# Grouped-query stages: where a step's softmax factors are finished, and how its values are shared out over four slots

## The chip, the cores and the metric

The kernel runs on one core of a Trainium2 chip as one launch. The core has five engines that work on their own instruction streams and meet through semaphores: TensorE (matrix products; its weight loads are shown apart), VectorE, ScalarE, GpSimd and SyncE, which here issues most of the DMA transfers. The metric is the device time of one execution in microseconds; less is better.

## The reference, cut to what matters

Four layers, each an attention over a context of 1601 positions and then a feed-forward part, on x of 4 x 256 x 256 in float32. Layers 1 and 3 have grouped-query attention: 16 query heads of width 128 that share 4 key/value heads. Layer 1 also attends to its own 256 positions and rotates queries and keys by position; layer 3 attends to the context alone:

```python
q = rms_norm((h @ Wq).reshape(B, S, 16, 128), q_norm_w)
k = rms_norm((e @ Wk).reshape(B, S_enc, 4, 128), k_norm_w)
v = (e @ Wv).reshape(B, S_enc, 4, 128)
k, v = jnp.repeat(k, 4, axis=2), jnp.repeat(v, 4, axis=2)
scores = jnp.einsum('bqhd,bkhd->bhqk', q, k) * 128**-0.5
probs = jax.nn.softmax(scores, axis=-1)
out = jnp.einsum('bhqk,bkhd->bqhd', probs, v).reshape(B, S, 16 * 128) @ Wo
```

The other stages (an attention that keeps the best 54 keys, mixtures of experts, a linear layer, an attention over image and text keys) are not touched.

## The kernel before, in words

The stages run one after the other. `gqa` is called twice, for layer 1 with rotation tables (`"l1a"`) and for layer 3 without them (`"l3a"`). Keys run in chunks of 128: 15 of them in the first (1857 keys), 13 in the second (1601); the last has 65.

A stage has 16 units (4 batches x 4 key/value heads); a unit has four steps (two blocks of 128 query positions x two pairs of heads). A step takes its scores in four slots, two score tiles in each. The order of the work is written out by hand: TensorE, ScalarE, VectorE and GpSimd get their instructions exactly in the order in which Python issues them. A loop over slots t issues the slot's scores (L1242) and then, phase by phase, what was put on that slot's lists:

```python
for phase in ("first", "early", "mid", "late", "last", "values", "pe", "post"):
    if phase == "mid" and rest:
        rest()
    for f in todo.pop((t, phase), ()):
        f()
```

Within a list the order is that in which entries were put there. The production of keys and queries (`begin`) is entered before the loop; `combine(i)` and `values(i)` are entered when the loop reaches t = 4i.

What one step i does, with its slots:

- Scores, slots 4i-4 to 4i-1: four products for four groups of 32 keys go into one of three PSUM score tiles (L1242). `rest` takes the negative maximum on VectorE (L1250) and the exponential with its sum on ScalarE (L1251). Each partition has a quarter of the keys, so a row's four quarters have maxima and sums of their own.
- Slot 4i: `turn` (L1264, TensorE) brings maxima and sums of the quarters onto 8 partitions; `top` takes the common maximum and the exponential of the difference (L1269, L1271 on VectorE, L1272 on ScalarE).
- Slot 4i+1: `total`, four small VectorE operations (L1276 to L1279), makes factors out of these; `back` (L1283, TensorE) turns the factors back; at the slot's end VectorE copies them (L1288) and GpSimd multiplies the first half of the step's exponentials by them (L1291, `scale(0)`). The second half follows in slot 4i+2.
- Slots 4i+3 and 4i+4: two block transposes on VectorE (L1296, `blocks`), in phase "last", write PT.
- Slots 4i+6 to 4i+9: the product of values and PT (L1322), chunk by chunk, into the one accumulator bank; slot 4i+10 copies it out on ScalarE (L1329), and after every second step the output projection follows (L1335).

So several steps overlap: the slot 4i+1 that has step i's `back` has the last part of the values of step i-2.

Beside this, keys, values and queries of the next unit are produced in the slots: projections (L1111, L1185) in phase "pe"; in the next slot "early" sums of squares on ScalarE (L1119, L1192), on VectorE ssq (queries, L1194) and rsq_t (L121), then the power on GpSimd (L122), and copies of V; "late" the scaling (L1127, L1202, L1206), in the first layer a slot later the rotation on GpSimd and VectorE (L1158 to L1160), then the transposes (L1137, L1217), and in the following slot, "early", the copies of KT and QT (L96 on VectorE, L98 on ScalarE, by turns). In the second stage the keys and values of the first batch and most of the second are loaded, not produced, so its slots have less TensorE work there.

PSUM has eight banks in these stages: three for scores, four (`tr`) for projections and transposes in rotation, one accumulator (`acc`).

Of the kernel before, what the change touches and what calls it, by code (L numbers as in the profile page):

```python
# [52 lines left out]
def kernel(ctx: ExitStack, tc: tile.TileContext, A, out: bass.AP):  # L53
# [5 lines left out]
    def ps_tile(shape, tag):  # L59
        return pools["ps"].tile(shape, F32, tag=tag, name=tag, bufs=pools[tag])  # L60
# [4 lines left out]
    def ps_tr():  # L65
        return ps_tile([P, 512], "tr")

    def ps_acc():
        return ps_tile([P, 512], "acc")

    def small(shape, tag, bufs=4):
        return sm.tile(shape, F32, tag=tag, name=tag, bufs=bufs)
# [107 lines left out]
    def residual(j, ps):  # L180
        nc.vector.tensor_tensor(X[j], ps, X[j], ALU.add)
# [383 lines left out]
    def sort_constants(pool):  # L565
        def table(shape, pattern, base, tag):
            t = pool.tile(shape, F32, tag=tag, name=tag)
            nc.gpsimd.iota(t, pattern, base=base, channel_multiplier=0, allow_small_or_imprecise_dtypes=True)
            return t

        k = dict(
            before=table([P, E], [[ROOM, E]], -1, "k_before"),
            first=table([P, E], [[ROOM, E]], P, "k_first"),
            step=table([P, E - 1], [[P, E - 1]], P, "k_step"),
            expert=table([P, E], [[1, E]], 0, "k_expert"),
            more=table([P, MORE], [[1, MORE]], 0, "k_more"),
            tri8=table([P, E, E], [[1, E], [-1, E]], 0, "k_tri8"),
        )
        nc.vector.tensor_scalar(k["tri8"], k["tri8"], 0.0, 1.0, ALU.is_ge, ALU.mult)
        k["tri"] = pool.tile([P, P], F32, tag="k_tri", name="k_tri")  # L580
        make_upper_triangular(nc, k["tri"], val=1.0, diag=True)
        k["ones"] = pool.tile([P, P], F32, tag="k_ones", name="k_ones")
        nc.gpsimd.memset(k["ones"], 1.0)
        return k
# [423 lines left out]
    def gqa(xT, key, tabs=None, early=None, others=None):  # L1008
        rope = tabs is not None
        ch = chunks(NCTX + (S if rope else 0))  # L1010
        nch = len(ch)
# [3 lines left out]
        W = nch * 32  # L1015
        lens = [sum(max(0, min(32, n - 32 * r)) for _, n in ch) for r in range(4)]
        pairs = [ch[i : i + 2] for i in range(0, nch, 2)]
        units = B * KVH
        steps = [(u, tt, pr) for u in range(units) for tt in range(2) for pr in range(2)]
        ET = mybir.EngineType  # L1020
        with (
# [11 lines left out]
            for i in range(3):  # L1033
                t = ps_tile([P, 512], f"sc{i}")
# [11 lines left out]
            def at(slot, phase, *fs):  # L1046
                todo.setdefault((slot, phase), []).extend(fs)
# [207 lines left out]
            def combine(i):  # L1255

                pes, ms = state.pop(steps[i])
                v = {}
                t = 4 * i

                def turn():
                    tr = ps_tr()
                    for k in range(2):
                        nc.tensor.transpose(tr[0:8, k * P : (k + 1) * P], ms[:, k, :], ident)  # L1264
                    v["m"], v["s"] = (tr[0:8, k * P : (k + 1) * P].rearrange("p (r t) -> p r t", r=4) for k in range(2))

                def top():
                    v["top"] = small([P, 32], "top", 2)[0:8]
                    nc.vector.tensor_reduce(v["top"], v["m"].rearrange("p r t -> p t r"), AX.X, ALU.min)  # L1269
                    v["f"] = pool.tile([P, 4, 32], F32, tag="cf", name="cf")[0:8]  # L1270
                    nc.vector.tensor_tensor(v["f"], v["top"].unsqueeze(1).to_broadcast([8, 4, 32]), v["m"], ALU.subtract)  # L1271
                    nc.scalar.activation(v["f"], v["f"], AF.Exp)  # L1272

                def total():
                    fs = pool.tile([P, 4, 32], F32, tag="cfs", name="cfs")[0:8]
                    nc.vector.tensor_tensor(fs, v["f"], v["s"], ALU.mult)  # L1276
                    nc.vector.tensor_reduce(v["top"], fs.rearrange("p r t -> p t r"), AX.X, ALU.add)
                    nc.vector.reciprocal(v["top"], v["top"])
                    nc.vector.tensor_tensor(v["f"], v["f"], v["top"].unsqueeze(1).to_broadcast([8, 4, 32]), ALU.mult)  # L1279

                def back():
                    v["tr"] = ps_tr()
                    nc.tensor.transpose(v["tr"][:, 0:8], v["f"].rearrange("p r t -> p (r t)"), ident[0:8, 0:8])  # L1283

                def scale(g):
                    if g == 0:
                        v["fac"] = small([P, 8], "fac", 2)
                        nc.vector.tensor_copy(v["fac"], v["tr"][:, 0:8])  # L1288
                    for a in range(4):
                        w = pes[g][:, a, :]  # L1290
                        nc.gpsimd.tensor_scalar(w, w, v["fac"][:, g * 4 + a : g * 4 + a + 1], 1.0, ALU.mult, ALU.mult)  # L1291

                def blocks(g):
                    if g == 0:
                        state[steps[i]] = pool.tile([P, nch, 2 * P], F32, tag="PT", name="PT")
                    nc.vector.transpose(  # L1296
                        state[steps[i]][:, :, g * P : (g + 1) * P].rearrange("p k (a t) -> p a k t", a=4),
                        pes[g].rearrange("p a (k i) -> p a k i", k=nch),
                    )

                at(t, "early", turn)
                at(t, "late", top)
                at(t + 1, "early", total)
                at(t + 1, "pe", back)
                at(t + 1, "post", lambda: scale(0))
                at(t + 2, "late", lambda: scale(1))
                at(t + 3, "last", lambda: blocks(0))
                at(t + 4, "last", lambda: blocks(1))

            def values(i):  # L1310
                u, tt, pr = steps[i]
                j = u // KVH * 2 + tt
                t = 4 * i + 6
                v = {}

                def part(q):
                    if q == 0:
                        v["ps"] = ps_acc()
                    V, PT = state[u]["V"], state[steps[i]]
                    for k in range(q * 4, min(q * 4 + 4, nch)):  # L1320
                        n = ch[k][1]
                        nc.tensor.matmul(  # L1322
                            v["ps"][:, 0 : 2 * P], V[:n, k, :], PT[:n, k, :], start=(k == 0), stop=(k == nch - 1)
                        )

                def out():
                    if pr == 0:
                        state["OT"] = pool.tile([P, GRP * P], F32, tag="OT", name="OT")
                    nc.scalar.copy(state["OT"][:, pr * 2 * P : (pr + 1) * 2 * P], v["ps"][:, 0 : 2 * P])  # L1329
                    del state[steps[i]]  # L1330

                def project():
                    v["ps"] = ps_tr()
                    for g in range(GRP):
                        nc.tensor.matmul(  # L1335
                            v["ps"][:, :D], state["OT"][:, g * P : (g + 1) * P], state[u]["wo"][:, g, :],
                            start=(g == 0), stop=(g == GRP - 1),
                        )

                for q in range(4):  # L1340
                    at(t + q, "values", lambda q=q: part(q))
                at(t + 4, "first", out)
                if pr:
                    at(t + 4, "pe", project)
                    at(t + 5, "early", lambda: residual(j, v["ps"][:, :D]))
# [6 lines left out]
            for u in range(units):  # L1352
# [7 lines left out]
                for g in range(n):  # L1360
                    t = t0 + (g // 2 if u == 0 else g * 12 // n)
# [5 lines left out]
            for t in range(-16, end):  # L1367
                i, q = divmod(t + 4, 4)
                rest = scores(i, q) if 0 <= i < len(steps) else None
                if q == 0 and 1 <= i <= len(steps):  # L1370
                    combine(i - 1)
                    values(i - 1)
# [5 lines that stand above are left out]
# [876 lines left out]
    with tc.tile_pool(name="sort", bufs=1) as sortp:  # L2254
        k = sort_constants(sortp)
# [4 lines left out]
    with rings(0, sc0=1, sc1=1, sc2=1, tr=4, acc=1):  # L2260
        gqa(layernorm(), "l1a", tabs)
# [6 lines left out]
    with tc.tile_pool(name="sort3", bufs=1) as sortp:  # L2268
        shw = sortp.tile([P, 3072], F32, tag="shw", name="shw")
        nc.sync.dma_start(shw, A["l3f_sw"])  # L2270
        with rings(0, sc0=1, sc1=1, sc2=1, tr=4, acc=1):
            xT = layernorm()
            k = sort_constants(sortp)
# [88 lines left out]
```

## Time and profile before

| | us |
|---|---|
| Median of 3 runs | 3859.56 |
| Lowest, highest | 3857.51, 3865.17 |
| The profiled execution's own time | 3858.06 |
| Its span, from the first to the last instruction | 3856.3 |
| First grouped-query stage, about | 523 to 1862 |
| Second grouped-query stage, about | 2638 to 3757 |

The durations that follow come from the profiled execution. PE is TensorE, PEld its weight loads, DVE VectorE, ACT ScalarE, POOL GpSimd. A float32 product is two matrix instructions in the trace, so eight L1322 instructions are four chunks. Instructions that follow each other on TensorE overlap, so the time of a block of them is read from its start to the next block's start. A line of a timeline gives start, length, engine, source line, operation, what is written from what, how many, and in brackets the idle time before it with what ended it.

### The profile page before, as it was taken

What the parts mean: (1) busy time and instruction counts of PE and PEld (TensorE: products, weight loads), DVE (VectorE), ACT (ScalarE), POOL (GpSimd) and SP (SyncE); (2) the same over time, 40 slices, a digit from 0 to 9 for tenths busy, and PEclk for the clock granted to TensorE, in tenths of its full rate; (3) what the DMA queues carried; (4) which work ended last, traced back from release to release, by engine and by line L of the source; (5) the groups of instructions that cost most, each with busy time, mean ns of one, the idle gap of its engine ahead of it and who ended that gap; (6) DMA issues with size and microseconds to landing.
All of it is one profiled execution on the core that took longest, in us unless ns stands there. A gap on an engine that the chain in (4) does not pass through costs nothing.

```text
span 3856.3 us, 63026 instructions
## 1 busy us (share of the span) xinstructions
PE 3603.5 (93%) x23397; PEld 2157.0 (56%) x23397; DVE 2611.3 (68%) x5142; ACT 1688.0 (44%) x4956; POOL 1310.3 (34%) x2091
## 2 busy tenths in 40 slices
PE   8887969999999999999899999987999999999998
PEld 4556944555565555555544454553555556556655
DVE  7884857777777777777665655525767767667664
ACT  4443635444454544444134444422433444444432
POOL 2332534454454444544310101012333333333422
PEclk9987979999999999999989999988999999999999
DMA  7326342222122222220100000033111111211104
GB/s 241 100 67 238 79 150 60 65 71 72 55 60 66 65 81 55 56 54 8 56 18 18 1 18 1 1 132 130 41 55 42 55 32 38 55 38 37 30 3 132
DMA packets 173715, 248.50 MB, mean 64 GB/s; under 512 B 21581, under 2 KB 134881, under 8 KB 169825
## 3 DMA queue, kind: packets, MB, share of 16 engines
q1 hardware_dynamic: 167025, 233.00, 19.5%
q0 software_dynamic: 6384, 11.47, 1.4%
q8 instruction: 186, 3.05, 0.3%
q14 instruction: 120, 0.98, 0.1%
HBM read 199.39 MB, written 45.03 MB: 63 GB/s over the span
## 4 chain that ended last, share of the span: by engine, by line
PE 64%; DVE 18%; POOL 7%; issue 5%; ACT 3%; DMA 3%; SPq 1%; POOLq 0%; DVEq 0%; ACTq 0%
PE acc L1322 15%; PE sc L1242 13%; PE tr L1111 5%; PE sc L1618 4%; DVE PT L1296 4%; PE sc L1572 3%; PE tr L1185 3%; PE acc L1639 3%; POOL pe L1291 3%; PE acc L884 2%; PE tr L1527 2%; PE tr L1335 2%; POOL t L1158 2%; DVE ms L1250 2%; ACT pe L1251 2%
## 5 line engine op out<-in xcount | busy, mean ns | idle before, releaser
L1251 ACT ACTIVATE pe<-sc,ms 128x480 f32<-128x480 f32 (+1 forms) x1024 | 644.0, 632 | 940.2 <-DVE ms L1250 922.9
L1322 PE MATMUL acc<-PT,V 128*128 128x256 f32 (+1 forms) x3584 | 898.4, 391 | 7.7 <-ACT OT L1329 7.2
L1242 PE MATMUL sc<-KT,QT 128*32 128x480 f32 (+5 forms) x8192 | 887.7, 535 | 14.2 <-ACT pe L1251 6.3
L1291 POOL TENSOR_SCALAR pe<-pe,fac 128x480 f32<-128x480 f32 (+1 forms) x1024 | 655.3, 660 | 613.4 <-ACT pe L1251 282.3
L1322 PEld LDWEIGHTS acc<-PT,V 128*128 128x128 f32 (+1 forms) x3584 | 643.2, 190 | 352.2 <-issue 182.1
L1250 DVE TENSOR_REDUCE ms<-sc 128x1 f32<-128x480 f32 (+1 forms) x1024 | 607.5, 615 | 173.3 <-PE sc L1242 147.2
L1296 DVE STREAM_TRANSPOSE PT<-pe 128x1920 f32<-128x1920 f32 (+1 forms) x256 | 519.5, 2030 | 0.0
L122 POOL TENSOR_TENSOR rs<-rsq_t,mhalf 128x2 f32<-128x2 f32 (+2 forms) x248 | 160.1, 646 | 863.8 <-DVE rsq_t L121 804.7
L1242 PEld LDWEIGHTS sc<-KT,QT 128*32 128x32 f32 x8192 | 218.1, 109 | 408.1 <-issue 309.2
L1111 PE MATMUL tr<-w,cx 128*128 128x256 f32 (+1 forms) x1264 | 303.5, 382 | 1.3 <-ACT nk L1127 1.3
L1624 ACT ACTIVATE pt<-sc 128x1024 f32<-128x1024 f32 (+1 forms) x224 | 214.1, 960 | 201.2 <-PE sc L1618 192.9
L1578 DVE TENSOR_REDUCE mx<-sc 128x2 f32<-128x1024 f32 (+1 forms) x192 | 207.2, 1089 | 114.8 <-PE sc L1572 65.5
L1618 PE MATMUL sc<-QT,KT 32*128 32x256 f32 (+1 forms) x1664 | 235.7, 405 | 21.2 <-DVE mx L1578 14.5
L1111 PEld LDWEIGHTS tr<-w,cx 128*128 128x128 f32 (+1 forms) x1264 | 226.7, 187 | 31.6 <-ACT nk L1127 2.0
L1572 PE MATMUL sc<-KT,QT 32*128 32x512 f32 (+2 forms) x1024 | 229.0, 553 | 0.7 <-DVE mx L1578 0.7
L1251 ACT ACTIVATION_READ_ACCUMULATOR pe<-sc,ms 128x1 f32 x1024 | 199.9, 195 | 0.0
L1618 PEld LDWEIGHTS sc<-QT,KT 32*128 32x128 f32 (+1 forms) x1664 | 136.5, 182 | 79.1 <-DVE mx L1578 51.2
L122 POOL TENSOR_TENSOR rsq<-rsq_t,mhalf 128x4 f32<-128x4 f32 x64 | 65.0, 1016 | 326.4 <-DVE rsq_t L121 326.4
L1119 ACT ACTIVATE sq<-tr 128x128 f32<-128x128 f32 (+1 forms) x348 | 97.1, 279 | 169.2 <-PE tr L1111 162.7
L121 DVE TENSOR_SCALAR rsq_t<-ss 128x2 f32<-128x2 f32 (+2 forms) x248 | 45.7, 185 | 172.1 <-ACT sq L1119 134.8
L1185 PE MATMUL tr<-w,xlnT 128*128 128x512 f32 x256 | 126.1, 618 | 4.4 <-DMA w<-in_l1a_wkv 3.2
L1572 PEld LDWEIGHTS sc<-KT,QT 32*128 32x128 f32 x1024 | 84.3, 190 | 76.6 <-issue 42.2
(430 smaller groups left out, 4849.1 us busy)
## 6 DMA issues: line engine op xcount, KB each, us to landing
cx<-in_ctxT SPq DMA_DIRECT2D x144, 256.0 KB, 3.1
tab<-rope SPq DMA_DIRECT2D x112, 256.0 KB, 2.7
w<-in_l0f_w SPq DMA_DIRECT2D x8, 2048.0 KB, 17.0
ctxT<-in_ctxT SPq DMA_DIRECT2D x7, 1601.0 KB, 6.4
w<-in_l2f_w SPq DMA_DIRECT2D x8, 1088.0 KB, 15.6
w<-in_l1a_wq SPq DMA_DIRECT2D x16, 512.0 KB
wo<-in_l1a_wo SPq DMA_DIRECT2D x16, 512.0 KB, 6.4
w<-in_l3a_wq SPq DMA_DIRECT2D x16, 512.0 KB, 7.1
```

What stands on the lines that cost most here:

```text
L122: nc.gpsimd.tensor_tensor(dst, t[:n, :k], mhalf[:n, :k], ALU.pow)
L1111: nc.tensor.matmul(v["ps"][:n, i, :], lhs, st["wkv"][:, c, :], start=(c == 0), stop=(c == NC_ - 1))
L1185: nc.tensor.matmul(v["ps"], xtok(xT, b * 2 + tt, c), state[u]["wq"][:, c, :], start=(c == 0), stop=(c == NC_ - 1))
L1242: nc.tensor.matmul(sc[32 * r : 32 * r + 32, 0 : lens[r]], st["QT"][:, tt, o : o + 32], st["KT"][:, r, 0 : lens[r]], start=True, stop=True,)
L1250: nc.vector.tensor_reduce(top, sc, AX.X, ALU.max, negate=True)
L1251: nc.scalar.activation(w, sc, AF.Exp, bias=top, accum_out=s)
L1291: nc.gpsimd.tensor_scalar(w, w, v["fac"][:, g * 4 + a : g * 4 + a + 1], 1.0, ALU.mult, ALU.mult)
L1296: nc.vector.transpose(state[steps[i]][:, :, g * P : (g + 1) * P].rearrange("p k (a t) -> p a k t", a=4), pes[g].rearrange("p a (k i) -> p ...
L1322: nc.tensor.matmul(v["ps"][:, 0 : 2 * P], V[:n, k, :], PT[:n, k, :], start=(k == 0), stop=(k == nch - 1))
L1572: nc.tensor.matmul(st[:, j, :n], QT[r, g, tt * P : (tt + 1) * P], KT[r, g, o : o + n], start=True, stop=True)
L1618: nc.tensor.matmul(st[:n, j, q, :], KT[r, g, o : o + n], QT[r, :], start=True, stop=True)
L1624: nc.scalar.activation(pt[:n, 2 * hp : 2 * hp + 2, :m], st[:n, :, :m], AF.Exp)
```

## The change

Two edits in `gqa`, so both stages have them. The order of phases, the buffers and the transfers are the same as before.

`total` is entered in phase "last" of slot 4i and no longer in phase "early" of slot 4i+1. `blocks(1)` of step i-1 was entered on the same list four slots before, so it comes ahead of `total` there. `back` stays in phase "pe" of slot 4i+1.

The chunks of a step's values are shared out by `cuts`. With 15 chunks, the slots 4i+6 to 4i+9 had 4, 4, 4, 3 and have 3, 4, 4, 4; with 13 they had 4, 4, 4, 1 and have 3, 3, 3, 4.

```diff
+        cuts = [q * (nch - 4) // 3 for q in range(4)] + [nch]
         units = B * KVH
...
                 at(t, "early", turn)
                 at(t, "late", top)
-                at(t + 1, "early", total)
+                at(t, "last", total)
                 at(t + 1, "pe", back)
...
                     V, PT = state[u]["V"], state[steps[i]]
-                    for k in range(q * 4, min(q * 4 + 4, nch)):
+                    for k in range(*cuts[q : q + 2]):
                         n = ch[k][1]
```

## The prediction

> **What bounds the kernel now.** I read the busy time by stage first, then the waits, then the timelines of TensorE and VectorE over a few steps. Only the two grouped-query stages run the changed lines. The busy table has columns of stretch, length, and busy time (instructions) of PE, PEld, DVE, ACT, POOL, then granted clock, DMA share and GB/s:
>
> ```profile
> 523.00:1862.00 1339.00, 1298.64 (x7893) 759.28 (x7893) 978.35 (x1813) 643.64 (x2193) 620.52 (x996) 0.99 0.22 63
> 2638.00:3757.00 1119.00, 1073.14 (x7064) 608.58 (x7065) 766.40 (x1594) 488.07 (x1605) 392.10 (x628) 0.99 0.15 46
> ```
>
> TensorE is busy for 97% and 96%, VectorE for 73% and 68%. So TensorE sets the length, and the change removes none of its work: it can win only time in which TensorE stands still. The list of waits (total us, times, longest) says where that is:
>
> ```profile
> PEld sc L1242 <- ACT pe L1251: 95.2, 134, 2.5
> ...
> PEld acc L1322 <- ACT OT L1329: 49.7, 57, 1.3
> ...
> PE tr L1283 <- DVE cf L1279: 36.6, 41, 3.0
> ```
>
> L1283 is the turning back of the factors, which waits for their last VectorE operation, L1279. The two rows above it are the scores that wait for a score bank, and the values that wait for the copy out of the single accumulator. One step of the second stage shows how they hang together, TensorE first, then VectorE:
>
> ```profile
> 3305.07 1.59 PE L1242 MATMUL sc<-KT,QT 128*32 128x416 f32 x16
> 3306.59 0.70 PE L1322 MATMUL acc<-PT,V 65*128 65x256 f32 x2
> 3307.99 0.20 PE L1283 MATMUL tr<-ident,cf 8*128 8x8 f32 x1 [0.70 <-DVE cf L1279]
> 3308.11 1.91 PE L1242 MATMUL sc<-KT,QT 128*32 128x416 f32 x16
> 3309.98 1.99 PE L1322 MATMUL acc<-PT,V 128*128 128x256 f32 x8
> 3311.90 1.59 PE L1242 MATMUL sc<-KT,QT 128*32 128x416 f32 x16
> ```
>
> ```profile
> 3304.20 1.89 DVE L1296 STREAM_TRANSPOSE PT<-pe 128x1664 f32<-128x1664 f32 x1
> 3306.03 0.14 DVE L96 COPY KT<-tr 128x32 f32<-128x32 f32 x1
> ...
> 3306.50 0.26 DVE L1276 TENSOR_TENSOR cfs<-cf,tr 8x128 f32<-8x128 f32 x1
> ...
> 3307.77 1.07 DVE L1250 TENSOR_REDUCE ms<-sc 128x1 f32<-128x416 f32 x2
> ```
>
> I number slots by their remainder mod 4, with t = 4i as slot 0. The first three PE lines are slot 1 (scores, one chunk of values, turning back), the next two slot 2. The values are 0.54 us of work, yet the next block starts 1.40 us after them: 0.86 us lost, of which the row shows 0.70 as a gap. Slot 2's scores take 1.87 us start to start where an undisturbed block takes 1.52: 0.35 lost more, because VectorE's reductions come after the factors, ScalarE's exponentials after these, and the accumulator's copy after these.
>
> **How much stands still.** The Trainium skill (Perfetto Trace Analysis, Identifying the Most-Contended Engine) says that matmul occupancy is no good measure of headroom. By the busy rows, idle time is 1339.00 - 1298.64 = 40 us and 1119.00 - 1073.14 = 46 us, start-up and end of the stages included. Counted instead from block start to block start against each block's undisturbed time, the stall before L1283 is 7.3 us in the first stage and 37.3 in the second, and that of slot 2's scores and the values behind them 16.8 and 18.1. Together 24.1 + 55.4 = 79.5 us, over 126 whole steps. I use these, since the stretched matmuls in the lines above bear the rule out: that is the ceiling of the gain. The first stage is nearly periodic: units 1 to 13 take 81.53 us each, with 1.2 us of this stall (0.10 + 0.80 in step 0, 0.33 in step 2). In the second, the units of the first two batches, whose keys are mostly loaded, have 1.4 to 11 us each, the later ones some 1.5 to 3.
>
> **The change, part by part.**
>
> *The factors' four operations move ahead* of the next slot's early work. They are means of 258, 363, 341 and 295 ns (L1276 to L1279), 1257 ns in all, 1.27 us in the lines above; the number of operations is unchanged.
>
> ```profile
> L1277 DVE TENSOR_REDUCE top<-cfs 8x32 f32<-8x128 f32 x128 | 46.4, 363 | 4.4
> ...
> L1276 DVE TENSOR_TENSOR cfs<-cf,tr 8x128 f32<-8x128 f32 x128 | 33.1, 258 | 0.5 <-ACT cf L1272 0.5
> ```
>
> They now come straight behind the second block transpose (L1296; it was put on slot 0's list four slots earlier, so it stays ahead). What they need, the exponential L1272, ends 1.2 to 1.75 us before that transpose does, apart from the first step of each stage: no new wait, thanks to the transpose's 1.9 to 2.2 us as cover. Without this cover it would be at most 0.4 us in each of 128 steps. What they pass is the early part of slot 1 on VectorE: copies of KT, QT or V, rsq_t, ssq. Between transpose and L1276 lie 37.7 us in the first stage and 76.5 in the second, of which 18.0 and 50.0 are idle. The idle part is mostly this:
>
> ```profile
> 3321.36 0.69 DVE L1194 TENSOR_REDUCE ssq<-sqq 128x4 f32<-128x512 f32 x1 [1.37 <-ACT sqq L1192]
> ...
> 3322.16 0.27 DVE L1276 TENSOR_TENSOR cfs<-cf,tr 8x128 f32<-8x128 f32 x1
> ```
>
> There the factors fit whole into a hole of 1.37 us, and slot 1's reductions come 1.3 us sooner too. Where VectorE has no hole, the reductions, which were behind the factors anyway, come no sooner or later; only the passed copies and rsq_t come up to 1.27 us later. Followed through a unit of the first stage: rsq_t would go from 1160.09 to about 1161.3, GpSimd's power and rotation (0.69 + 0.92) end at 1163.0 instead of 1161.9, VectorE's rotation at 1162.63 waits 0.4 us, and slot 2's reductions start near 1164.3 instead of 1163.81. The scores which need these banks start at 1168.26. I cost it at nothing for that margin; if it were gone, it would be up to 1.27 us a step.
>
> *The values are cut anew*: 4, 4, 4, 3 chunks in the first stage become 3, 4, 4, 4 in slots 2, 3, 0, 1; in the second 4, 4, 4, 1 become 3, 3, 3, 4. A chunk is 1.73 / 4 = 0.43 us. No matmul is added. In front of L1283, slot 1 gains 0.43 us in the first stage and 3 x 0.43 = 1.29 in the second, as cover for the factors; the slots before it lose 0 and 0.86. One chunk in each stage goes from behind slot 2's stall to ahead of it: 0.43 us of stall filled per step wherever there is that much. The 0.86 lets slots 0 and 1 begin sooner, which helps as far as VectorE was waiting for scores there.
>
> No DMA, no queue of SP, no bank or buffer allocation moves. GpSimd's scaling starts when L1283 is done; the block transposes that read it have never waited (their idle time is 0.0), and with slots 2 and 3 shorter by 0.86 they keep about 2 us: 2 x 2.36 us of scaling against some 5 us until the first transpose needs half of it.
>
> **The sum.** In the step shown, from slot 0's start at 3301.45: TensorE reaches L1283 at 3.62 - 0.43 + 1.52 + 1.83 = 6.54 us, the factors are done by about 5.9, so no stall. Slot 2's scores would end at 6.67 + 1.52 = 8.19; the copy of the accumulator, behind the exponentials as before, is done at 8.5, which is when values started before (8.53). After that slot 2 and slot 3 are each a chunk shorter: 0.86 saved of 1.21 lost. So the rule for a step is the smaller of its stall and 0.43 plus what VectorE gains.
>
> First stage: VectorE gains nearly nothing in the steps with a stall. Smaller of stall and 0.43, over the steps: 12.5 us (12.9 with gains). Second stage: 18.4 us if only the chunk counts, 40.2 if every hole and every earlier start is used in full. The nine steps with the 1.43 us hole for ssq should get their whole 1.38, the eight like the one worked out 0.86 instead of 1.2 or more: 40.2 less about 3 is 37, I take 36. Sum: 48.5 us. 3858.06 (the profiled execution; its span is 3856.3) - 48.5 = 3809.6; the median of the runs lies 1.5 higher, so **3811 us**.
>
> A rule against it: the same page (Optimization Strategy) says that a consistently repeating gap can mean too few PSUM buffers. Here it would be the single accumulator and the three score banks (the 49.7 and 95.2 us rows), which stay. By that rule the stall of L1283 merely reappears in slot 2, and only the moved chunk helps: 31 us. The worked step has both: its OT wait grows to 0.3 us, and 0.86 is saved still. So I take the trace, with the rule as the next case.
>
> **Rivals and chances.** *The forecast* (35 to 60 us saved): 0.50. *Only the chunk*: the stall moves on to the scores and the accumulator, 12.5 + 18.4 = 31 us saved, 3829 us: 0.25. For it: VectorE has no hole in first-stage steps; against it: 50 us of holes in the second. *All stall gone*: 79 us, 3780: 0.07. *A wash* within 0.2% (7.7 us, about what a measurement can tell from no change: the three runs spread by that): new stalls in slots 3 and 0, shorter by a chunk each while VectorE has transposes of 1.9 us in both and now the factors, 3.2 and 4.9 us against 2.9 and 3.3 of TensorE without production: 3855: 0.07. *Slower*, by one mechanism: the passed rsq_t comes late, and with it GpSimd's power, ScalarE's scaling, and keys' transposes on TensorE. In 94 of the steps there is work that is passed (44 and 50 by stage); at 1.27 us each that is 119 us against 48.5 won, about 3930 us; it decides from 0.52 us a step. Against it: the 3 us and more in hand above. 0.11.
>
> So faster 0.82, same 0.07, slower 0.11. The range 3790 to 3848 holds the forecast, the second case and part of the wash; it leaves out most of "all gone" and the slower case. The forecast's own range is 3798 to 3825.
>
> **What would show it.** Right: the wait of L1283 for L1279 falls from 36.6 to under 5 us; cfs follows PT directly; the second stage is 30 to 40 us shorter, the first 10 to 15; the first's period goes from 81.53 to about 80.8. Wrong: scores waiting for pe or values for OT grow by what L1283 loses (then it is the second case); L1137 waiting for nk, or a longer first stage (then the slower one).

## The result and the profile after

The changed kernel takes 3823.99 us (median of 5 runs, 3819.20 to 3827.38) against 3859.56. The ratio is 0.9906, with a 95% interval of 0.9892 to 0.9919: about 36 us saved, 31 to 42. The forecast was 3811, its range 3790 to 3848.

To see where they come from, I measure each stage from its first scores (L1242) to the start of the values (L1322, L1324 after) that follow its last output projection but one, and a unit from its first slot 0 to the next unit's:

| us | before | after | difference | forecast |
|---|---|---|---|---|
| First stage (with rotation) | 1286.6 | 1282.5 | -4.1 | -12.5 |
| One unit of it, units 1 to 13 | 81.53 | 81.33 | -0.20 | about -0.76 |
| Second stage | 1088.4 | 1055.3 | -33.0 | -36 |
| Stall before the turning back, second stage | 37.3 | 11.6 | -25.7 | |
| Stall in slot 2's scores and before the values, second stage | 15.9 | 9.9 | -6.0 | |

(The last row counts the scores' block alone; the prediction's 18.1 also had 2.2 us behind it.) Behind the mark that ends a stage here some 12 and 10 us of values follow, with one chunk more in the new cut; to the end of the last values the differences are -3.7 and -32.6. Of the first stage's 4.1 us, 2.1 are in its last unit, which has no production beside it.

A part of this is TensorE's clock and not the stalls. In the kernel before, the granted clock reads 0.50 for 3.4 us in the second stage and for 3.4 us in the last unit of the first; after, neither stretch is there. These are the two rows of the busy table (the granted clock is the third number from the end), and the values inside the second of them:

```profile
2816.10:2819.50 3.40, 3.40 (x14) 1.99 (x7) 0.77 (x2) 1.79 (x7) 3.40 (x7) 0.50 0.17 72
1850.10:1853.50 3.40, 3.40 (x9) 2.75 (x9) 0.17 (x1) 0.00 (x0) 3.00 (x5) 0.50 0.00 0
...
1850.06 3.68 PE L1322 MATMUL acc<-PT,V 128*128 128x256 f32 x8
```

Eight such instructions take 1.99 us elsewhere. The two stretches cost some 1.6 and 1.7 us, which the change saves and the forecast didn't have. (A stretch of 6.8 us in the second stage's first unit is in every kernel here.)

The busy table by stage after, with the columns of the one before (stretch, length, PE, PEld, DVE, ACT, POOL, granted clock, DMA share, GB/s):

```profile
523.00:1858.00 1335.00, 1297.01 (x7893) 757.95 (x7894) 974.99 (x1812) 641.70 (x2193) 620.18 (x995) 0.99 0.22 63
2634.00:3720.00 1086.00, 1063.40 (x7061) 609.17 (x7062) 762.31 (x1600) 495.67 (x1604) 394.29 (x635) 0.99 0.16 48
```

The instructions are the same; what went is time around them, and in the second stage some of TensorE's busy time, in which a matrix instruction that is stretched over a wait or runs at the lower clock counts whole. The list of waits after (lines have moved by two; us in total, times, longest):

```profile
DVE nk L1161 <- POOL t L1160: 99.6, 103, 2.3
PEld sc L1244 <- ACT pe L1253: 75.4, 98, 2.5
DVE nq L1161 <- POOL t L1160: 64.0, 32, 2.5
PEld acc L1324 <- ACT OT L1331: 50.8, 59, 1.3
...
PE tr L1285 <- DVE cf L1281: 9.7, 9, 2.4
```

The turning back waits 9.7 us for the factors and no longer 36.6; the scores wait less, the accumulator as before. Two rows have grown: VectorE waits for t, the rotation on GpSimd, which is in the first stage alone. They stood in the same list of before, and the prediction did not cite them:

```profile
DVE nk L1159 <- POOL t L1158: 81.7, 68, 2.1
...
DVE nq L1159 <- POOL t L1158: 48.9, 32, 1.9
```

The step worked out in the prediction, after the change, first TensorE, then VectorE. Its slot 0 starts at 3272.46:

```profile
3277.17 2.00 PE L1324 MATMUL acc<-PT,V 128*128 128x256 f32 x8
3279.10 0.22 PE L1285 MATMUL tr<-ident,cf 8*128 8x8 f32 x1
3279.25 1.79 PE L1244 MATMUL sc<-KT,QT 128*32 128x416 f32 x16
3281.00 1.56 PE L1324 MATMUL acc<-PT,V 128*128 128x256 f32 x6
```

```profile
3275.22 1.89 DVE L1298 STREAM_TRANSPOSE PT<-pe 128x1664 f32<-128x1664 f32 x1
3277.05 0.23 DVE L1278 TENSOR_TENSOR cfs<-cf,tr 8x128 f32<-8x128 f32 x1
...
3278.08 0.28 DVE L1281 TENSOR_TENSOR cf<-cf,top 8x128 f32<-8x128 f32 x1
...
3278.79 1.08 DVE L1252 TENSOR_REDUCE ms<-sc 128x1 f32<-128x416 f32 x2
```

The factors follow the transpose directly and end about 5.9 us into slot 0's time; TensorE comes to L1285 at 6.64 us and doesn't wait; slot 2's values start at 8.54 us, practically as before (8.53). From slot 0 to the next slot 0 it is 13.05 us instead of 13.90: 0.85 us saved.

### The profile page after: what moved, and what is told of

The parts are those of the page before. It is cut to its first block, busy times and chain, and to the rows that moved or that the text cites. A ratio compares the mean times of both kernels' runs of the same rounds, so it can differ in the third digit from the quotient of the medians.

```text
span 3821.5 us, 63032 instructions
## 1 busy us (share of the span) xinstructions
PE 3593.1 (94%) x23397; PEld 2156.9 (56%) x23397; DVE 2601.9 (68%) x5142; ACT 1694.6 (44%) x4956; POOL 1309.4 (34%) x2091
## 4 chain that ended last, share of the span: by engine, by line
PE 68%; DVE 14%; POOL 7%; issue 4%; DMA 2%; ACT 2%; SPq 1%; POOLq 0%; DVEq 0%; ACTq 0%
PE acc L1324 16%; PE sc L1244 15%; PE tr L1113 5%; PE sc L1620 4%; PE sc L1574 3%; PE acc L1641 3%; PE tr L1187 3%; POOL pe L1293 3%; DVE PT L1298 3%; PE acc L884 2%; POOL t L1160 2%; PE tr L1337 2%; PE tr L1529 2%; DVE mx L1580 1%; DVE m L521 1%
## 5 line engine op out<-in xcount | busy, mean ns | idle before, releaser
L1324 PE MATMUL acc<-PT,V 128*128 128x256 f32 (+1 forms) x3584 | 896.0, 390 | 7.0 <-ACT OT L1331 7.0
L1244 PE MATMUL sc<-KT,QT 128*32 128x480 f32 (+5 forms) x8192 | 882.3, 534 | 15.9 <-ACT pe L1253 12.1
L1324 PEld LDWEIGHTS acc<-PT,V 128*128 128x128 f32 (+1 forms) x3584 | 641.5, 190 | 349.8 <-issue 205.8
L1161 DVE TENSOR_TENSOR nk<-nk,tab 128x256 f32<-128x256 f32 (+1 forms) x128 | 65.7, 513 | 101.2 <-POOL t L1160 99.6
```

Source lines behind the costliest of these rows:

```text
L1244: nc.tensor.matmul(sc[32 * r : 32 * r + 32, 0 : lens[r]], st["QT"][:, tt, o : o + 32], st["KT"][:, r, 0 : lens[r]], start=True, stop=True,)
L1324: nc.tensor.matmul(v["ps"][:, 0 : 2 * P], V[:n, k, :], PT[:n, k, :], start=(k == 0), stop=(k == nch - 1))
```

## The experiments

The stage lengths of all runs, in us, from one profiled execution each:

| | first stage | its unit | second stage | kernel, median |
|---|---|---|---|---|
| before | 1286.6 | 81.53 | 1088.4 | 3859.6 |
| after | 1282.5 | 81.33 | 1055.3 | 3824.0 |
| factors alone | 1286.6 | 81.45 | 1081.9 | 3855.0 |
| values alone | 1281.7 | 81.36 | 1055.6 | 3826.5 |
| after, less scaling | 1264.5 | 80.30 | 1055.8 | 3809.1 |
| before, less scaling | 1279.0 | 81.13 | 1088.5 | 3854.0 |
| one chunk from behind | 1282.0 | 81.34 | 1064.1 | one run |
| two chunks from ahead | 1283.5 | 81.28 | 1067.2 | one run |
| two quarters on ScalarE | 1265.2 | 80.30 | 1056.0 | 3807.4 |
| rotation first | 1309.0 | 83.19 | 1055.7 | 3851.4 |
| ScalarE, factors as before | 1264.0 | 80.29 | 1055.2 | 3805.9 |
| ScalarE, five chunks | 1264.3 | 80.29 | 1051.3 | 3804.1 |

A stage that an edit doesn't touch repeats to about 1.5 us, a unit of the first stage to some 0.05. The kernel before had medians of 3860.0 to 3861.3 beside these runs; the ratios below are against those.

**The two edits apart.** The first keeps the factors' new place and the old cut:

```diff
-                    for k in range(*cuts[q : q + 2]):
+                    for k in range(q * 4, min(q * 4 + 4, nch)):
```

> Only the factors are moved ahead; the values stay cut 4, 4, 4, 3 and 4, 4, 4, 1. Theory A (in the first stage the chunk that went ahead of the turning back delays the factors' copy, GpSimd's scaling behind it and the rotation that VectorE waits for, so its gain is given back): a unit of the first stage takes 81.4 to 81.6 us here, against 81.53 before and 81.33 after. Rival B (what costs the first stage its gain is the passed rsq_t, 1.27 us later, and with it GpSimd's power and rotation): 81.7 to 82.0 us a unit, longer than before. Both: second stage 12 to 22 us shorter than before; whole kernel 3838 to 3850 us by A, 3845 to 3855 by B.

Measured: ratio 0.9982 (0.9976 to 0.9989), 6 us. The first stage is unchanged, its unit 0.08 us shorter: rival B's longer unit is refuted. The second stage wins 6.5 us where 12 to 22 were expected, and the kernel is slower than theory A's 3838 to 3850. Step by step, the nine steps of the second stage with a hole before ssq win 1.26 us each, as the prediction reasons. The eight steps like the worked one win nothing: in one of them the stall before the turning back falls from 0.87 to 0.38 us, and that of slot 2's scores grows from 0.34 to 0.85. Over the stage the first falls from 37.3 to 19.0 and the second grows from 15.9 to 22.1.

TensorE's clock takes back about half of the gain. In the second stage four steps have a stretch at 0.50, by which they are 1.6, 1.6, 2.9 and 1.7 us longer; the kernel before has one there, in another step, of 1.6. The longest, as a row of the busy table and on TensorE:

```profile
3518.70:3525.50 6.80, 6.14 (x24) 3.66 (x27) 2.19 (x6) 2.86 (x9) 4.72 (x8) 0.50 0.00 0
...
3519.36 1.60 PE L1244 MATMUL sc<-KT,QT 128*32 128x416 f32 x8 [1.91 <-ACT pe L1253]
3520.89 3.78 PE L1324 MATMUL acc<-PT,V 128*128 128x256 f32 x8
```

Without these stretches, by an estimate from the lengths of the steps, the factors alone would have won about 13 us in the second stage.

The second keeps the new cut and puts the factors back:

```diff
-                at(t, "last", total)
+                at(t + 1, "early", total)
```

> Only the values are cut anew; the factors stay in the next slot's early phase. Theory A: a unit of the first stage takes 81.2 to 81.5 us, since the later turning back gives the moved chunk's gain back. Rival B: 80.7 to 80.9 us, the 0.43 + 0.33 us of stall in steps 0 and 2 filled by the chunk. Both: second stage 18 to 30 us shorter than before; whole kernel 3830 to 3842 us.

Measured: ratio 0.9912 (0.9899 to 0.9926). **The cut alone gives nearly all**: second stage 32.8 us shorter (18 to 30 were expected), first stage 4.9. Theory A's unit of 81.2 to 81.5 us is met with 81.36. Against the full change the difference in both stages is under 1 us. So the factors' move, for which the prediction had a good part of its sum, adds nothing beside the cut: in the second stage, stalls of 16.4 us before the turning back and 5.3 in slot 2's scores are left with the cut alone, 11.6 and 9.9 with both.

Why, one step of the second stage shows in which TensorE gets to the turning back before the factors even with four chunks ahead. First the values' cut alone, then the full change; both timelines are TensorE's:

```profile
3204.49 2.00 PE L1324 MATMUL acc<-PT,V 128*128 128x256 f32 x8
3207.59 0.19 PE L1285 MATMUL tr<-ident,cf 8*128 8x8 f32 x1 [1.10 <-DVE cf L1281]
3207.71 1.91 PE L1244 MATMUL sc<-KT,QT 128*32 128x416 f32 x16
3209.58 1.56 PE L1324 MATMUL acc<-PT,V 128*128 128x256 f32 x6
```

```profile
3202.59 2.00 PE L1324 MATMUL acc<-PT,V 128*128 128x256 f32 x8
3204.51 0.22 PE L1285 MATMUL tr<-ident,cf 8*128 8x8 f32 x1
3204.66 0.89 PE L1244 MATMUL sc<-KT,QT 128*32 128x416 f32 x8
3206.84 0.89 PE L1244 MATMUL sc<-KT,QT 128*32 128x416 f32 x8 [1.29 <-ACT pe L1253]
3207.70 1.56 PE L1324 MATMUL acc<-PT,V 128*128 128x256 f32 x6
```

The stall of 1.10 us before L1285 is gone, and one of 1.29 us stands in the middle of the scores. From the values' start to the next values' start it is 5.09 us with the one and 5.11 with the other. The reason is in VectorE's timeline of the full change:

```profile
3203.50 0.28 DVE L1281 TENSOR_TENSOR cf<-cf,top 8x128 f32<-8x128 f32 x1
3203.70 0.41 DVE L1956 BATCH_NORM_STATS2 bnst<-x 128x6 f32<-128x256 f32 x1
...
3205.48 1.08 DVE L1252 TENSOR_REDUCE ms<-sc 128x1 f32<-128x416 f32 x2
```

The work that the factors passed (here the statistics of the next stage's normalization) now stands between the factors and slot 1's reductions. The reductions release, through the exponentials, the score bank that slot 2 needs, and they start when factors and passed work are both done, in whichever order: 7.6 us after slot 0's start in both.

**What took the first stage's gain.** Theory A: a chunk ahead of L1285 makes the factors' copy later, then GpSimd's scaling, and the rotation that stands behind it in GpSimd's queue. The first stage's largest stall, 0.80 us in slot 2 of a unit's step 0, hangs on the step ahead of it, the last of the unit before. There slot 2's rotation, on GpSimd (POOL) and then on VectorE, looks like this before:

```profile
1143.38 1.41 POOL L1158 TENSOR_TENSOR t<-nq,tabq 128x256 f32<-128x256 f32 x2
...
1144.83 1.15 DVE L1159 TENSOR_TENSOR nq<-nq,tabq 128x512 f32<-128x512 f32 x1 [1.81 <-POOL t L1158]
```

and after:

```profile
1142.70 1.42 POOL L1160 TENSOR_TENSOR t<-nq,tabq 128x256 f32<-128x256 f32 x2
...
1144.16 1.15 DVE L1161 TENSOR_TENSOR nq<-nq,tabq 128x512 f32<-128x512 f32 x1 [2.55 <-POOL t L1160]
```

Counted from this step's slot 0 (1128.78 before, 1127.69 after), the delay goes through undiminished from TensorE to the reductions that free the next step's score banks. The last two columns are experiments that follow:

| us from slot 0 | before | after | less scaling | rotation first |
|---|---|---|---|---|
| Slot 2's scores, behind the turning back (TensorE) | 10.60 | 11.03 | 11.03 | 11.03 |
| Copy of the factors (VectorE) | 10.71 | 11.13 | 11.13 | 11.13 |
| Slot 2's rotation (GpSimd) | 14.60 | 15.01 | 13.87 | 13.61 |
| Slot 2's rotation (VectorE) | 16.05 | 16.47 | 15.32 | 15.06 |
| Slot 3's rotation (VectorE) | 21.52 | 21.96 | 20.81 | 23.11 |
| Block transpose (VectorE) | 22.86 | 23.30 | 22.14 | 24.45 |
| Slot 1's reductions in the next step (VectorE) | 32.71 | 33.09 | 31.94 | 34.25 |
| Stall of slot 2's scores in the next step | 0.80 | 0.75 | 0.00 | 1.5 |

So the chunk goes ahead by 0.43 us, and what would free the banks comes 0.38 us later. To test it I took work out of GpSimd's queue, in the changed kernel and as a control in the kernel before. This leaves two quarters of each first half unscaled:

```diff
-                    for a in range(4):
+                    for a in range(2 if rope and g == 0 else 4):
                         w = pes[g][:, a, :]
```

> The changed kernel; in the first stage two of the four multiplications of each first half's scaling on GpSimd are left out (1.3 us of its queue a step; two quarters of the exponentials stay unscaled, so this is a look at time only). Theory A: the rotation that VectorE waits for comes up to 1.3 us sooner in slots 2 and 3, the stall of 0.33 us in step 2 goes and that of step 0 shrinks: a unit takes 80.6 to 81.0 us against 81.33. Rival C (the stall in slot 2 is held up by the three score banks and the one accumulator alone, GpSimd has no part): 81.2 to 81.4 us.

> The same two multiplications left out of the kernel before, as the control. Theory A: the stall of step 2 shrinks here too, 80.9 to 81.3 us a unit against 81.53. Rival C: 81.5 us.

Measured: 80.30 us a unit in the changed kernel, even less than theory A's 80.6 to 81.0, and 81.13 in the kernel before, where it is step 0's stall that shrinks (0.80 to 0.40 us) and not step 2's. Rival C is refuted: with banks and accumulator as they are, slot 2's scores lose 3.5 us in the whole stage instead of 17.2 (16.8 in the kernel before). VectorE's operations don't run faster for it (the block transpose takes 2163 ns in both, the rotation's product of 128 x 512 920 and 919), so it is the waiting that goes. The difference between the two kernels, 0.83 us a unit, is what the change is worth in the first stage once GpSimd's queue is shorter; the prediction's rule gave 0.76. With the queue as it is, 0.20 are left.

**A part of the cut at a time.** In the second stage alone:

```diff
+        if not rope:
+            cuts = [0, 3, 7, 11, 13]
```

> The changed kernel with 3, 4, 4, 2 chunks in the second stage: only the chunk that lay behind slot 2's stall goes ahead of it, and slots 3 and 0 keep their four. By the prediction's rule (the smaller of the stall and 0.43 us a step, which is 18.4 us over the stage) the second stage is 18 to 23 us shorter than before (1088.4 us), with the little that the factors add. Rival (what counts is the cover in front of the turning back, one chunk of three): a third of the 33 us, so 11 to 14.

```diff
+        if not rope:
+            cuts = [0, 4, 7, 10, 13]
```

> The changed kernel with 4, 3, 3, 3 chunks in the second stage: slots 3 and 0 give one each to slot 1, slot 2 keeps four. No TensorE work changes its side of slot 2's stall; the gain can come only from scores of slots 0 and 1 that begin sooner for VectorE (0.45 us of waiting for them in most steps). By the prediction's rule the second stage is 12 to 20 us shorter than before. Rival (the cover in front of the turning back counts, two chunks of three): 22 to 26.

Measured: 24.3 and 21.2 us shorter than before (23.8 and 21.2 to the end of the last values). The rival's 11 to 14 for the first is refuted; the rule's 18 to 23 is missed by a little. The second lies just above the rule's 12 to 20 and below the rival's 22 to 26, so it doesn't decide. Step by step the two parts are worth nearly the same: each shortens the eight steps like the worked one by 0.42 us, and both together by 0.85. In the nine steps with the hole each wins 1.26 us, which the factors alone win too; so the two stage gains have these 11 us in common and don't add up to 45.5. Most of the second's arrears, 1.7 us, is one more stretch at the clock of 0.50.

**A better version.** The two multiplications go to ScalarE, so all is computed:

```diff
+                def scale_act():
+                    for a in range(2, 4):
+                        w = pes[0][:, a, :]
+                        nc.scalar.activation(w, w, AF.Copy, scale=v["fac"][:, a : a + 1])
...
+                if rope:
+                    at(t + 2, "late", scale_act)
                 at(t + 2, "late", lambda: scale(1))
```

> The changed kernel; in the first stage two of the four multiplications of each first half's scaling go from GpSimd to ScalarE, in the late phase of slot 2, so all is computed. By theory A (GpSimd's queue behind the factors' copy sets the first stage's stalls) a unit takes 80.3 to 80.7 us against 81.33, and the kernel 3806 to 3814 us. If ScalarE's 1.3 us a step delay the exponentials of slot 3 and the copies behind them: 81.3 us or more.

Measured: 3807.4 us, ratio 0.9865 (0.9849 to 0.9882); 80.30 us a unit, as when the work was left out. ScalarE's added 1.3 us a step cost nothing that shows. Slot 2 of a unit's step 0 on TensorE, first in the changed kernel, then in this one:

```profile
1161.20 2.05 PE L1244 MATMUL sc<-KT,QT 128*32 128x480 f32 x16
1163.68 1.56 PE L1324 MATMUL acc<-PT,V 128*128 128x256 f32 x6 [0.43 <-ACT OT L1331]
```

```profile
1155.39 1.80 PE L1244 MATMUL sc<-KT,QT 128*32 128x480 f32 x16
1157.13 1.56 PE L1331 MATMUL acc<-PT,V 128*128 128x256 f32 x6
```

The scores take 1.74 us from start to start, as undisturbed ones do, and 2.48 in the changed kernel.

Is it the queue's length or only the rotation's place in it? In the next, the first half's scaling stands behind slot 2's rotation, and nothing is taken off:

```diff
+                if rope:
+                    at(t + 2, "late", lambda: multiply(0))
                 at(t + 2, "late", lambda: scale(1))
```

> The changed kernel; in the first stage the first half's scaling stands behind slot 2's rotation in GpSimd's queue, directly ahead of the second half's; nothing is taken off the queue. By theory A VectorE's wait for the rotation in slot 2 (about 2 us) goes, the one in slot 3 stays or grows, because GpSimd starts later and has the same work: 81.0 to 81.6 us a unit. If only the rotation's place behind the scaling mattered, not the queue's length: 80.3 to 80.6 us.

Measured: 83.19 us a unit, 1.9 us longer than after, outside of both expectations. So the place isn't the remedy. The table above shows why: slot 2's rotation does come sooner, but both halves' scaling then stands in one piece of 6.02 us ahead of slot 3's rotation on GpSimd, for which VectorE waits 2.87 us (1.71 after), and all that follows in the table is 1.2 us later than after.

Last, the factors back in their old place in that better version, and one more chunk ahead in the second stage:

```diff
-                at(t, "last", total)
+                at(t + 1, "early", total)
```

> The kernel with two quarters on ScalarE, but the factors back in the next slot's early phase. If the factors' place is worth little once the chunks stand in front of the turning back, in the first stage too: a unit within 0.15 us of 80.30, second stage 1055 to 1056.5 us, kernel within 4 us of 3807. If GpSimd's queue had hidden their worth in the first stage: 80.6 us or more a unit, kernel 3811 us or more.

```diff
+        if not rope:
+            cuts = [0, 2, 5, 8, 13]
```

> The kernel with two quarters on ScalarE and 2, 3, 3, 5 chunks in the second stage: one more chunk goes from behind slot 2's stall to ahead of it. By the prediction's rule it fills up to 0.43 us in the steps that still have a stall (21.5 us over the stage, about 9 us of it in the first batch): second stage 3 to 8 us shorter than 1055.3. If the later turning back delays the scaling until block transposes wait: 1056 us or more.

Measured: 3805.9 us with the old factors, ratio 0.9859 (0.9843 to 0.9875), 80.29 us a unit: their place is worth nothing in the first stage either. Five chunks: 3804.1 us, ratio 0.9853 (0.9836 to 0.9869), second stage 4.7 us shorter than with four (4.2 to the end of the last values). This is the fastest of all kernels run, some 20 us faster than the changed one. The two were not tried together.

## Why the prediction was right, and where it was not

**TensorE sets the length, and only its stalls can be won.** Right in the main: the two stages got shorter by 37.1 us with the same instructions on TensorE. But 3.3 us of this are the stretches at half the clock, a term that the forecast did not have.

**The second stage, 36 us.** Right in size: 33.0 us, 1.6 of it the clock. The worked step saved 0.85 us against 0.86, the nine steps with a hole 1.26 each against 1.38. The rule "the smaller of the stall and 0.43 plus what VectorE gains" holds for these steps; for the two parts of the cut it came out 1 us too low at its upper ends.

**The factors' move, part of that sum.** Here a step of the reasoning failed, though not the number: the nine steps were to get their 1.38 us by way of the factors filling the hole. They do with the factors alone, but the cut alone gives them the same 1.26, since three more chunks ahead cover the stall, of which under 0.1 us is left before L1285: both edits fill one and the same stall. Where VectorE has no hole, moving the factors gives the stall to slot 2's scores, as the step above shows. The prediction had said that "the reductions, which were behind the factors anyway, come no sooner or later", and didn't draw the conclusion that the scores' stall then stays. The factors' move alone gives 6 us, and on top of the cut nothing that can be measured.

**The first stage, 12.5 us.** Wrong: 4.1 us, 1.7 of it the clock in the last unit. The step that failed is "One chunk in each stage goes from behind slot 2's stall to ahead of it: 0.43 us of stall filled per step". It held VectorE's schedule fixed while L1285 was moved 0.43 us later. The prediction looked at GpSimd's scaling only for the block transposes, which never waited, and not for the rotation behind it, for which VectorE did wait: 130.6 us in two rows of its own list. With two multiplications taken off that queue the rule's 0.76 us a unit appear as 0.83.

**The signs.** The wait of L1283 for L1279 fell to 9.7 us, not under 5, and the first stage's period to 81.33, not to 80.8. The factors follow PT directly, and no wait for pe or OT grew by what L1283 lost, as forecast.

**The passed rsq_t.** The expected 0.4 us of waiting for the rotation in slot 1 is there, 0.53 us, in the step that the prediction followed:

```profile
1162.50 0.43 DVE L1161 TENSOR_TENSOR nk<-nk,tab 128x256 f32<-128x256 f32 x1 [0.53 <-POOL t L1160]
```

With the factors alone a unit still gets 0.08 us shorter, so it costs nothing there, as forecast; the slower rival had no ground.

**The rule on PSUM buffers.** Its place was right for the steps in which VectorE's reductions come late: what is left of the stall does stand in slot 2's scores. But the runs show that most of it can be filled without more buffers: chunks ahead of it in the second stage and a shorter GpSimd queue in the first did so with the same banks. More banks weren't tried.

**Where in the range.** 36 us saved lies at the lower end of the forecast's own case (35 to 60). Without the 3.3 us of the clock it would be about 32, beside the second case's 31: that the own case was met at all is luck. It is still not the second case, which had 18.4 us for the second stage and 12.5 for the first. The missing 12 us are 8.4 in the first stage and 3.0 in the second; the rest is within what the runs' medians vary.

## What to carry to other kernels

In this schedule a stall was filled by independent work of the same engine, moved ahead of the wait. Finishing the awaited result sooner helped only where the engine that makes it had a hole; where it passed other work on that engine, the stall moved to the next consumer. If two edits fill the same stall, count it once. Before work is put ahead of an instruction, follow everything that this instruction releases through every queue to the next wait, the slow engine's queue above all, and look for that wait in the list of before. To find which of several in-order queues holds a pipeline back, shorten one of them by leaving work out: it takes one run, and here moving the work elsewhere then gave the same. Look at the granted clock before a longer step is put down to waits.

## What was unexpected of the hardware

TensorE's granted clock fell to 0.50 for 3.4 to 6.8 us behind waits that add up to 1.5 to 2.1 us (1.29 and 0.18, 1.59, and 0.21 and 1.91 us in the three stretches shown), and its matrix instructions took about twice as long. It does not follow from the waits alone: in the run with the factors alone, another step with waits of 0.21 and 1.90 us kept its clock of 1.00. What decides is not shown.

ScalarE took over two 128 x 480 multiplications a step with no effect on the unit's length that shows (80.30 us with them, 80.30 with them left out). Operations on 8 partitions and at most 128 elements take 0.23 to 0.36 us on VectorE, and the first of the four took 0.23 us directly behind the transpose where it had mostly taken 0.27 before.
